# A second result buffer for the early expert tiles, one set of PSUM banks for Mamba, experts and results, and row fetches ahead of weight loads

## Chip, core and metric

The kernel runs on one core of a Trainium2 chip. A core has five engines with queues of their own: TensorE (PE: matmuls, with its weight loads listed as PEld), VectorE (DVE), ScalarE (ACT), GpSimd (POOL) and SyncE (SP), which here issues most of the DMAs. PE writes its products to PSUM, eight banks of 512 float32 columns on 128 partitions; DVE and ACT read them there. The metric is the device time of one execution in microseconds. Names such as L1825 are line numbers of the kernel before.

## What is computed

The input is a float32 image tensor of 2 x 256 x 48 x 48. Layer 0 is a hybrid of a 7 x 7 neighbourhood attention and dynamic depthwise convolutions. Its output is taken as 2 x 2304 = 4608 tokens of 256 features, and layer 1 is a Mamba block followed by a mixture of eight experts, of which each token uses two. The part that matters here, cut from the reference:

```python
t = _to_tokens(x)
t = t + _L1_attn_ref(_ln_t(t), ...)          # Mamba
t = t + _L1_ffn_ref(_ln_t(t), ...)           # experts
x = _from_tokens(t, x)

def _L1_ffn_ref(x, Wg, bg, W1, b1, W2, b2):
    gate_logits = xf @ Wg + bg
    top_w, top_i = jax.lax.top_k(gate_logits, 2)
    top_w = jax.nn.softmax(top_w, axis=-1)
    for e in range(8):
        h = jax.nn.gelu(xf @ W1[e] + b1[e], approximate=False)
        out = out + w_dense[:, e:e + 1] * (h @ W2[e] + b2[e])
```

W1 is 256 x 1024 and W2 1024 x 256 for each expert.

## The kernel before

**Order of the work.** `run` goes through four stages: layer 0, Mamba with the gate, the experts, and the results. Layer 0 and Mamba are put in order by a planner, `Flow`. Each operation is given an engine, a cost, the operations it needs, and the buffers that it takes and frees; `room` tells how many buffers of each kind there are. The planner walks through time with these costs and writes one order for PE, DVE, ACT and SP. POOL's order is kept by `on_pool`. Behind the plan, semaphores make each instruction wait for its data and for its buffer, so the engines run in the planned order but not at planned times. The experts and the results are written as plain loops.

**Mamba and the gate.** 36 chunks of 128 tokens run through Mamba. A finished chunk's tokens lie in `x` on chip; a copy goes to DRAM in `acc` (the keep, L1505), where the experts' rows are added later. The gate works on groups of chunks. For each chunk it normalizes the tokens (L1664) and POOL scatters them, once for each of the two chosen experts, into a table `xs` in DRAM that is sorted by expert (the row puts, L1673, an indirect DMA each). A row holds 256 features, eight weights and the token's number.

**Early tiles.** Before the gate has seen every chunk, the kernel takes the expert with most tokens so far and runs three tiles of 256 of its rows, numbered 0 to 2, beside Mamba (`early_tile`). One tile is: a fetch of its rows (L1762), four PE transposes (L1771), a copy to SBUF (L1787), W1 products in four pairs (L1799), GELU on ACT (L1807), W2 products (L1815) summed in one bank, the sum with the bias on DVE (L1825), the scaling by the expert weight on ACT (L1831), and two scatters that add 128 rows each to `acc`, issued by POOL (L1834). The expert weight comes from POOL (L1775) and DVE (L1783). The tile's input, hidden values and result lie in columns of `x[1]` whose tokens are done with. There is one result buffer (`ey=1` in `room`): columns 768 to 1023.

**Plan of the rest.** When all counts are known, `plan` computes on DVE (L1863 to L1926) which rows and which expert each of the remaining tiles has. Its scratch values lie in `x[1]` from column 1024 on (`begun`).

**Experts.** 33 pair tiles of 256 rows and four single tiles of 128 rows follow (four more singles stand in a branch for unusual counts). Tile i needs `load(i)`, SP's DMAs of 136 KB (`bt`) and 2 MB (`wt`) of weights (L1979, L1981; tile 0 has its weights in `x[0]` already), and `fetch(i)`, SP's DMA of its rows (L1989). The first of them stand on SP's queue in the order load 1, fetch 0, fetch 1, load 2, fetch 2, behind eight DMAs that fill the ends of the table. `turn` transposes the rows on PE (L897), copies them on DVE (`ext`, L899), and takes the token numbers and weights. `up` makes 32 matmuls (L2045) with a GELU per bank (L2049). `down` of a pair tile makes seven products of 128 x 128 blocks (L2083), Strassen's scheme, whose operand sums `ts` and `ss` DVE has made (L2019 to L2034); then ACT copies the first product (L2087), DVE sums the products (L2088 to L2096), ACT scales (L2054), and POOL scatters and adds to `acc` (L2055). A single tile has plain products (L2070).

**Results.** After the last scatter has landed, `acc` is read back in 12 pieces (L2147), transposed on PE (L2158), copied by DVE and ACT (L2161) and written out (L2164).

**PSUM.** Layer 0 has its own pool. Mamba has six banks that the planner hands out (`bank`) and a pool of two for the z products (`zbank`). The experts open two new pools in place of Mamba's: four single banks, and two sets of two banks for the products of `down`. The results open the same two again. A new pool in the place of an old one can be used when the old one's last users are done:

```python
def psum(self, ctx, bank, banks):
    self.ps = self.pool("ps", bank, ctx, space=bass.MemoryType.PSUM)
    self.ps2 = self.pool("ps2", banks, ctx, space=bass.MemoryType.PSUM)
```

Of the kernel before, what the change touches and what calls it, by code (L numbers as in the profile page):

```python
# [31 lines left out]
F32 = mybir.dt.float32  # L32
I32 = mybir.dt.int32
AF = mybir.ActivationFunctionType
# [3 lines left out]
P = 128  # L38
B, C, H, W = 2, 256, 48, 48
N = H * W  # L40
NH = C // P
# [26 lines left out]
NCHUNK = B * NBLK * NJ  # L68
# [5 lines left out]
TR = 256  # L74
# [152 lines left out]
class Kernel:  # L227
# [4 lines left out]
    def pool(self, name, bufs, ctx=None, **kw):  # L232
        return (ctx or self.ctx).enter_context(self.tc.tile_pool(name=name, bufs=bufs, **kw))

    def bank(self):
        return self.ps.tile([P, 512], F32, tag="bank", name="bank")

    def banks(self):
        return self.ps2.tile([P, 2, 512], F32, tag="banks", name="banks")

    def psum(self, ctx, bank, banks):
        self.ps = self.pool("ps", bank, ctx, space=bass.MemoryType.PSUM)
        self.ps2 = self.pool("ps2", banks, ctx, space=bass.MemoryType.PSUM)


    def setup(self):
# [70 lines left out]

    def bank_for(self, key):
        slot = self.flow.slot["bank", key]
        t = self.tiles["bank", key] = self.ps.tile([P, 512], F32, tag=f"bank{slot}", name="bank")  # L320
        return t

    def banks_for(self, key):
# [5 lines left out]
    def layer0(self, ctx):  # L329


        nc, ins = self.nc, self.ins
        self.ps = self.pool("ps", 1, ctx, space=bass.MemoryType.PSUM)
        wts = self.pool("l0w", 1, ctx)
        room = dict(bank=4, banks=2, q=2, prob=3, pt=4, val=3, vout=2, hid=2, place=2)
        self.begin_flow(self.pool("att", 1, ctx), room, self.PACE0, self.LEAD0)
        self.kp = [wts.tile([P, HP, HP], F32, name=f"kp{h}") for h in range(NH)]
        self.xp = {(b, h): wts.tile([P, H, W], F32, name=f"xp{b}{h}") for b in range(B) for h in range(NH)}
        self.prepare(wts)
        self.scale_weights()  # L340
        for b in range(B):
            self.group_norm(b)
            for g in range(-(-H // KG)):
                self.keys(b, g)
            for rb in range(NRB):
                self.queries(b, rb)
            for pair in range(N // (2 * P)):
                self.values(b, pair)
            self.convolutions(b)
            for i in range(NBQ):  # L350
                self.block(b * NBQ + i)
        self.run_flow()
# [560 lines left out]
    def mamba(self, ctx):  # L913

        nc = self.nc
        self.ps = self.pool("ps", 1, ctx, space=bass.MemoryType.PSUM)
        self.zps = self.pool("zps", 2, ctx, space=bass.MemoryType.PSUM)

        room = dict(bank=6, zbank=2, cvbank=2, t=3, xn=2, xc=2, bc=3, cz=2, z=2, btt=2, xd=3, xw=2,
                    mt=4, yi=1, y=4, sq=2, state=3, rd=2, u2=2, ex=1, ext=1, ehid=2, ey=1)
        self.begin_flow(self.pool("m", 1, ctx), room, self.PACE1, self.LEAD1)
        zeros = self.pool("cz", 1, ctx)
        self.cz = [zeros.tile([P, 2, TB], F32, name=f"cz{i}") for i in range(room["cz"])]
        for t in self.cz:
            nc.gpsimd.memset(t, 0.0)
        for k in range(B * NBLK):
            self.norms(k)
            self.project_block(k)  # L930
            self.decays_of(k)
            for c in range(k * NJ, (k + 1) * NJ):
                self.chunk(c)
        first = 0
        for g, n in enumerate(GROUPS):
            self.gate(g, first, n)
            first += n
        self.early_expert(sum(GROUPS[: EARLY + 1]))
        for i in range(NEARLY):
            self.early_tile(i, sum(GROUPS[: EARLY + 1]))  # L940
        self.run_flow()
# [248 lines left out]
    def decays_of(self, k):  # L1190
# [54 lines left out]
        for i in range(NZ):  # L1245
            at = (k, i)

            def gate(i=i, at=at):
                if i == 0:
                    self.large_tile("z", k, [P, NZ, TB])  # L1250
                T["zbank", at] = self.zps.tile([P, 512], F32, tag="zbank", name="zbank")
                self.project(
                    T["zbank", at][:, :TB], lambda h: win[:, h, i * P : (i + 1) * P], lambda h: T["xn", k][:, h, 3:]
                )

            op(("z", at), "PE", 1300, gate, *rows, ("z", (k, i - 1)) if i else None,
               takes=[("zbank", at)] + ([("z", k)] if i == 0 else []), uses=[("xn", k)])
# [483 lines left out]
    def early_tile(self, i, seen):  # L1741
# [4 lines left out]
        w1 = wt[:, : NH * HID].rearrange("p (k o) -> p k o", k=NH)  # L1746
        w2 = wt[:, NH * HID :].rearrange("p (k o) -> p k o", k=NHC)
        late = NCHUNK + 6 + i
        xt, hid, y = (self.x[1][:, :, a * TR : b * TR] for a, b in ((0, 1), (1, 3), (3, 4)))
        free = [(name, c) for c in (NCHUNK // 2 + 6, NCHUNK // 2 + 7) for name in ("u2", "keep")]  # L1750
        sp = [mybir.EngineType.SP]
        puts = [("put", (c, q)) for c in range(seen) for q in range(2)]
        weights = [("ew", (0, q)) for q in range(8)]
# [68 lines left out]
               takes=[("bank", ("ed", i))] if p == 0 else [], uses=[("ehid", (i, p))])  # L1822

        def add():
            self.last_add = vec.tensor_tensor(y, T["bank", ("ed", i)].rearrange("p (j q) -> p j q", j=2),  # L1825
                              bcast(bt[:, NHC : NHC + C], 1, [P, 2, C]), ALU.add)

        op("ea", "DVE", 690, add, ("ed", (i, NHC // 2 - 1)), *free, takes=[("ey", i)], uses=[("bank", ("ed", i))])
        for j in range(2):
            def scale(j=j):  # L1830
                nc.scalar.activation(y[:, j, :], y[:, j, :], AF.Identity, scale=T["eweight", i][:, j : j + 1])  # L1831

            def put(j=j):
                ins = pool.indirect_dma_start(  # L1834
                    self.acc, bass.IndirectOffsetOnAxis(ap=T["etoken", i][:, j : j + 1], axis=0), y[:, j, :],
                    None, compute_op=ALU.add,
                ).ins
                self.tc.declare_no_dep(ins, group="early", reason="a token has one row of an expert")
                self.tc.declare_no_dep(ins, group="late keeps", reason="later chunks have other rows")
                self.tc.add_to_no_dep_group("early", ins)  # L1840

            op(("es", (i, j)), "ACT", 390, scale, ("ea", i), ("eweight", i))
            op(("eput", (i, j)), "POOL", 1500, put, ("es", (i, j)), ("etoken", i), *[("keep", c) for c in range(seen)],
               uses=[("ey", i)])

    def plan(self):

        nc, begun = self.nc, [4 * TR] * NH
        n, k, tid = P, CAP // TR, self.c["tid"]
        tri = self.c["tri"].rearrange("p (a b) -> p a b", a=E)  # L1850

# [91 lines left out]

    def experts(self, ctx):
        nc, ins = self.nc, self.ins
        self.psum(ctx, 4, 2)
        hp = self.pool("eh", 2, ctx)
        ew = self.pool("ew", 3, ctx)
        sp = [mybir.EngineType.SP]
# [111 lines left out]
        def down(i):  # L2061
            wt, bt, hid = *weights[i], hidden[i]
            w2 = wt[:, NH * HID : NH * HID + NHC * C].rearrange("p (k o) -> p k o", k=NHC)
            b2 = bt[:, NHC : NHC + C]
            banks = self.ps2.tile([P, 2, 512], F32, tag="banks", name="po")
            if tiles[i][0] == 1:
                y = hp.tile([P, C], F32, tag="ey", name="ey", bufs=5)
                po = banks[:, 0, :C]
                for c in range(NHC):
                    nc.tensor.matmul(po, lhsT=hid[:, c, :P], rhs=w2[:, c, :], start=c == 0, stop=c == NHC - 1)  # L2070
                nc.vector.tensor_add(y, po, b2)
                finish(i, y, 0)
            else:
                v = sums.pop(i)
                p = {}

                for n, (name, a, w) in enumerate((
                    (1, "a11", "b11"), (7, "s3", "t3"), (2, "a12", "b21"), (4, "a22", "t4"), (5, "s1", "t1"),
                    (6, "s2", "t2"), (3, "s4", "b22"),
                )):  # L2080
                    p[name] = banks[:, n // 4, n % 4 * P : (n % 4 + 1) * P]
                    for c in range(NHC // 2):
                        nc.tensor.matmul(p[name], lhsT=v[a][:, c], rhs=v[w][:, c], start=c == 0, stop=c == NHC // 2 - 1)  # L2083
                y0, y1 = (hp.tile([P, C], F32, tag="ey", name="ey", bufs=5) for _ in range(2))
                p1, u2, u3, u4 = (hp.tile([P, P], F32, tag=f"u{j}", name=f"u{j}", bufs=1) for j in range(4))
                add = nc.vector.tensor_add
                nc.scalar.copy(p1, p[1])  # L2087
                add(y0[:, :P], p[2], p1)  # L2088
                add(u2, p[6], p1)
                add(u3, p[7], u2)  # L2090
                add(u4, p[5], u2)
                add(y1[:, :P], p[4], u3)
                add(y1[:, P:], p[5], u3)
                add(y0[:, P:], p[3], u4)
                for j, y in enumerate((y0, y1)):
                    add(y, y, b2)  # L2096
                    finish(i, y, j)
# [3 lines left out]
        for e in range(E):  # L2101
            fill(e)
        load(0)
        load(1)
        fetch(0)
        fetch(1)
        load(2)
        fetch(2)
        with self.tc.issue_after(self.last_add.ins):
# [26 lines left out]
    def results(self, ctx):  # L2136

        nc = self.nc
        self.psum(ctx, 4, 2)
        op = self.pool("o", 12, ctx)  # L2140

        blocks = []
# [156 lines left out]
```

## Time and profile before

| | |
|---|---|
| median of 3 runs | 1323.94 us (1323.86 to 1324.54) |
| the profiled execution | 1323.21 us, of which the span from first to last instruction is 1321.3 us |
| PE busy | 1237.3 us (94%) |
| DVE, ACT, POOL busy | 930.1, 796.4, 557.2 us |
| mean granted PE clock | 0.979 |

The stages around the change, from the trace's table of windows:

| stretch (us) | what runs there | PE busy | granted clock | DMA share |
|---|---|---|---|---|
| 765.0 to 783.5 | end of the gate, early tiles 1 and 2 | 18.31 | 1.00 | 0.55 |
| 783.5 to 794.5 | early tile 2 | 0.00 | 0.73 | 1.07 |
| 794.5 to 806.0 | early tile 2, hand-over | 9.94 | 0.81 | 0.45 |
| 806.0 to 1236.0 | expert tiles | 429.82 | 1.00 | 0.66 |
| 1236.0 to 1284.0 | last expert tiles | 47.76 | 1.00 | 0.41 |
| 1284.0 to 1293.0 | last sums and scatters | 0.00 | 0.67 | 0.25 |
| 1293.0 to 1321.3 | results | 12.22 | 0.74 | 0.89 |

Times in the trace count from the first instruction. A row of a timeline gives the start, the duration, the engine, the line, the operation with its output and inputs, and in brackets how long the engine stood idle before it and what ended that. The granted clock is the share of full speed at which PE could run. A DMA share of 1 means that the core's sixteen DMA engines were all busy (packets that overlap can take it over 1).

### The profile page before, as it was taken

To read this page: it belongs to the slowest core of one execution; us is meant where nothing else is said; L and a number is where in the kernel's file an instruction comes from. 1 tells how busy PE (TensorE), PEld (TensorE's weight loads), DVE (VectorE), ACT (ScalarE), POOL (GpSimd) and SP (SyncE) were. 2 spreads that over 40 slices of the span, in tenths; PEclk is the share of its full clock that TensorE was granted. 3 is DMA by queue.
4 is the path that set the end of the run, shared out by engine and by line. 5 is a ranking of instruction groups with operands and counts; after the bars stand their busy time and mean duration, and the time that the engine had idled before them with its cause. 6 is when DMAs were issued, how large, how long until landed. Compare 5 with 4: busy or idle time off the path is not lost. (4 is left out here: it accounts for less than half of the span.)

```text
span 1321.3 us, 23603 instructions
## 1 busy us (share of the span) xinstructions
PE 1237.3 (94%) x8072; PEld 984.5 (75%) x8072; DVE 930.1 (70%) x2427; ACT 796.4 (60%) x1957; POOL 557.2 (42%) x769
## 2 busy tenths in 40 slices
PE   4999999996999999999999968999999999999983
PEld 3566766664667766677677757999999999999982
DVE  5899999998577978888878634565556556555642
ACT  2598868897899887987787623333324333332332
POOL 4312130211367798988889852212212221221220
PEclk9999999999899999999999999999999999999997
DMA  8331322210232342426346165667756765775618
GB/s 293 108 102 47 118 72 89 63 49 30 70 93 83 88 139 86 142 80 191 114 137 179 59 213 172 177 193 229 238 176 226 230 210 183 233 236 183 217 33 295
DMA packets 101659, 194.13 MB, mean 147 GB/s; under 512 B 10635, under 2 KB 82652, under 8 KB 96604
## 3 DMA queue, kind: packets, MB, share of 16 engines
q1 hardware_dynamic: 84156, 166.15, 37.3%
q0 software_dynamic: 14400, 19.74, 7.6%
q10 hardware_dynamic: 2980, 6.69, 1.4%
q8 instruction: 66, 1.08, 0.3%
q14 instruction: 57, 0.47, 0.1%
HBM read 154.24 MB, written 43.23 MB: 149 GB/s over the span
## 5 line engine op out<-in xcount | busy, mean ns | idle before, releaser
L2055 POOL DMA_INDIRECT acc<-ey,token x70 | 109.0, 1558 | 371.7 <-ACT ey L2054 331.1
L2045 PE MATMUL bank<-ext,wt 128*128 128x256 f32 (+1 forms) x1152 | 241.3, 368 | 0.0
L2045 PEld LDWEIGHTS bank<-ext,wt 128*128 128x128 f32 x1152 | 207.0, 190 | 25.0
L2049 ACT ACTIVATE hid<-bank,bt 128x256 f32<-128x256 f32 (+1 forms) x288 | 132.3, 461 | 84.9 <-PE bank L2045 80.2
L2087 ACT COPY u<-po 128x128 f32<-128x128 f32 x33 | 8.8, 266 | 205.8 <-PE po L2083 200.0
L676 POOL COPY kp<-kp 128x10 f32<-128x10 f32 (+1 forms) x60 | 24.7, 412 | 179.5 <-DVE kp L669 179.5
L587 DVE SCALAR_TENSOR_TENSOR x<-hid,w2r,x 128x1128 f32<-128x1128 f32 (+3 forms) x72 | 99.9, 1393 | 0.4 <-ACT hid L581 0.2
L2083 PE MATMUL po<-ts,ss 128*128 128x128 f32 x792 | 99.2, 275 | 0.0
L911 PE MATMUL bank<-xn,win 128*128 128x387 f32 x240 | 93.0, 511 | 1.6 <-ACT t L993 1.6
L2083 PEld LDWEIGHTS po<-ts,ss 128*128 128x128 f32 x792 | 93.7, 192 | 0.0
L1123 DVE SCALAR_TENSOR_TENSOR xc<-bank,vec,xc 128x384 f32<-128x384 f32 x144 | 86.6, 611 | 9.2 <-ACT xc L1112 8.6
L1339 ACT ACTIVATE mt<-mt,cum 128x128 f32<-128x128 f32 x288 | 87.7, 393 | 0.0
L795 ACT ACTIVATE prob<-prob,top 128x308 f32<-128x308 f32 x144 | 78.2, 550 | 15.4 <-DVE top L784 15.0
L1673 POOL DMA_INDIRECT xs<-u,rows x72 | 72.5, 1008 | 16.0 <-issue 13.8
L2019 DVE TENSOR_TENSOR ts<-wt 128x512 f32<-128x512 f32 x32 | 22.2, 692 | 80.8 <-PE po L2083 80.8
L2032 DVE TENSOR_TENSOR ss<-hid 128x512 f32<-128x512 f32 x33 | 22.8, 691 | 72.8 <-ACT hid L2049 72.8
L1445 PE MATMUL bank<-wout,y 128*128 128x264 f32 x288 | 71.6, 393 | 1.2 <-DVE yi L1404 1.2
L911 PE MATMUL zbank<-xn,win 128*128 128x384 f32 x192 | 71.0, 491 | 0.3 <-ACT z L1241 0.3
L801 ACT ACTIVATE prob<-prob,rden 128x308 f32<-128x308 f32 x144 | 67.6, 549 | 3.7 <-DVE rden L850 3.7
L577 DVE SCALAR_TENSOR_TENSOR hid<-xp,vec,hid 128x1175 f32<-128x1175 f32 (+1 forms) x48 | 68.4, 1425 | 0.1
L2083 PE MATMUL po<-wt,hid 128*128 128x128 f32 x512 | 67.6, 275 | 0.0
L784 DVE CUSTOM_DVE_ANT_0 prob<-banks,cst 128x308 f32<-128x308 f32 x144 | 61.7, 472 | 4.9 <-PE banks L774 4.6
(324 smaller groups left out, 3017.7 us busy)
## 6 DMA issues: line engine op xcount, KB each, us to landing
wt<-in_We SPq DMA_DIRECT2D x36, 2048.0 KB
mt<-decays SPq DMA_DIRECT2D x36, 512.0 KB
ex<-xs SPq DMA_DIRECT2D x36, 265.0 KB
rd<-decays SPq DMA_DIRECT2D x68, 128.0 KB
val<-vtab SPq DMA_DIRECT2D x72, 110.0 KB
bt<-in_We SPq DMA_DIRECT2D x36, 136.0 KB
vraster<-vout SPq DMA_DIRECT2D x18, 256.0 KB
acc<-x SPq DMA_DIRECT2D x36, 128.0 KB
```

The source lines that it names most:

```text
L577: nc.vector.scalar_tensor_tensor(dst, src, w[:, k : k + 1], dst, ALU.mult, ALU.add)
L587: nc.vector.scalar_tensor_tensor(dst, src, w[:, k : k + 1], dst, ALU.mult, ALU.add)
L795: nc.scalar.activation(t, t, AF.Exp, bias=T["top", c][:, a : a + 1], scale=-1.0, accum_out=T["den", c][:, a : a + 1])
L911: self.nc.tensor.matmul(ps, lhsT=lhs(k), rhs=rhs(k), start=k == 0, stop=k == NH - 1)
L1123: nc.vector.scalar_tensor_tensor(out(), T["bank", ("cv", at)][:, i : i + TB], wc[:, i : i + 1], out(), ALU.mult, ALU.add)
L1339: nc.scalar.activation(t, t, AF.Relu, bias=at_s, scale=-1.0)
L1445: nc.tensor.matmul(ps[:, : C + E], lhsT=T["y", c][:, m, :], rhs=self.l1["wout"][:, m, :], start=m == 0, stop=m == NZ - 1,)
L1673: ins = nc.gpsimd.indirect_dma_start(self.xs, bass.IndirectOffsetOnAxis(ap=of("rows")[:, i, q : q + 1], axis=0), T["u2", g][:, i, :], None,)
L2045: nc.tensor.matmul(ps[:, :rows], lhsT=w1[:, k, c * P : (c + 1) * P], rhs=xt[:, k, :], start=k == 0, stop=k == NH - 1,)
L2049: nc.scalar.activation(hid[:, c, :], ps[:, :rows], AF.Gelu, bias=bt[:, c : c + 1])
L2055: put = nc.gpsimd.indirect_dma_start(self.acc, bass.IndirectOffsetOnAxis(ap=token[:, j : j + 1], axis=0), y, None, compute_op=ALU.add)
L2083: nc.tensor.matmul(p[name], lhsT=v[a][:, c], rhs=v[w][:, c], start=c == 0, stop=c == NHC // 2 - 1)
```

## The change

The change has three parts.

1. **Two result buffers.** `room` has `ey=2`. The planner gives each early tile one of two slots in `x[1]`, columns 768 to 1023 or 1024 to 1279; the tiles take them in the order first, second, first. Tiles 1 and 2 also need chunks 26 and 27, whose columns the second slot covers, to be done with. The plan's scratch begins at column 1280.
2. **One set of banks.** Mamba's pool now lives to the end, with the two `zbank` as banks of it that the planner hands out. A list `used_banks` keeps the banks in the order in which they were last used. The experts take the four that were used longest ago for transposes and `up`, and the other four for `down`: two for a pair tile, one for a single tile. The results go on with the same four. The two banks of a pair tile are now two tiles and no longer one of twice the size. The first four products of `down` (1, 7, 2, 4) lie in the first, the other three (5, 6, 3) in the second, as before.
3. **Order on SP.** Fetch 0, fetch 1, load 1, load 2, fetch 2.

In the order of the instructions, PE's is the same up to the results. On DVE the weight L1783 of tile 2 moves one place ahead; behind tile 2's sum comes `ext` of the first expert tile, ahead of its `own`, `token` and first `ts`; and in each pair tile the first sum of products (L2088) comes ahead of the next tile's first two `ts`. A memset of the plan moves back by some places. In the results one block changes places with its neighbour on PE and ACT.

```diff
+    def next_bank(self, ring, name):
+        tag = ring.pop(0)
+        ring.append(tag)
+        return self.ps.tile([P, 512], F32, tag=tag, name=name)
+
     def bank(self):
-        return self.ps.tile([P, 512], F32, tag="bank", name="bank")
...
-    def psum(self, ctx, bank, banks):
-        self.ps = self.pool("ps", bank, ctx, space=bass.MemoryType.PSUM)
-        self.ps2 = self.pool("ps2", banks, ctx, space=bass.MemoryType.PSUM)
+        return self.next_bank(self.ring, "bank")
+
+    def share_banks(self):
+
+        self.ring, self.sums = self.used_banks[:4], self.used_banks[4:]
...
         slot = self.flow.slot["bank", key]
-        t = self.tiles["bank", key] = self.ps.tile([P, 512], F32, tag=f"bank{slot}", name="bank")
+        t = self.tiles["bank", key] = self.next_bank([f"bank{slot}"], "bank")
+        self.used_banks = [tag for tag in self.used_banks if tag != f"bank{slot}"] + [f"bank{slot}"]
...
-        self.ps = self.pool("ps", 1, ctx, space=bass.MemoryType.PSUM)
-        self.zps = self.pool("zps", 2, ctx, space=bass.MemoryType.PSUM)
+        self.ps = self.pool("ps", 1, space=bass.MemoryType.PSUM)
+        self.used_banks = ["zbank0", "zbank1"]
...
-                    mt=4, yi=1, y=4, sq=2, state=3, rd=2, u2=2, ex=1, ext=1, ehid=2, ey=1)
+                    mt=4, yi=1, y=4, sq=2, state=3, rd=2, u2=2, ex=1, ext=1, ehid=2, ey=2)
...
-                T["zbank", at] = self.zps.tile([P, 512], F32, tag="zbank", name="zbank")
+                T["zbank", at] = self.next_bank([f"zbank{self.flow.slot['zbank', at]}"], "zbank")
...
-        free = [(name, c) for c in (NCHUNK // 2 + 6, NCHUNK // 2 + 7) for name in ("u2", "keep")]
+        free = [(name, NCHUNK // 2 + c) for c in (6, 7, 8, 9)[: 2 + 2 * (i > 0)] for name in ("u2", "keep")]
...
         def add():
+            at = 3 + self.flow.slot["ey", i]
+            y = T["ey", i] = self.x[1][:, :, at * TR : (at + 1) * TR]
             self.last_add = vec.tensor_tensor(y, T["bank", ("ed", i)].rearrange("p (j q) -> p j q", j=2),
...
-        nc, begun = self.nc, [4 * TR] * NH
+        nc, begun = self.nc, [5 * TR] * NH
...
-        self.psum(ctx, 4, 2)
+        self.share_banks()
...
-            banks = self.ps2.tile([P, 2, 512], F32, tag="banks", name="po")
+            banks = [self.next_bank(self.sums, "po") for _ in range(tiles[i][0])]
...
-                    p[name] = banks[:, n // 4, n % 4 * P : (n % 4 + 1) * P]
+                    p[name] = banks[n // 4][:, n % 4 * P : (n % 4 + 1) * P]
...
         load(0)
-        load(1)
         fetch(0)
         fetch(1)
+        load(1)
         load(2)
         fetch(2)
...
     def results(self, ctx):
 
         nc = self.nc
-        self.psum(ctx, 4, 2)
```

## Prediction

> **What bounds the kernel now.** I read the page first: PE is busy 1237.3 us of a span of 1321.3 us, so what can be won is idle PE time and slow PE time. Then the table of windows (columns: busy time and instructions of PE, PE loads, DVE, ACT, POOL; then granted clock, DMA share, GB/s), cut at the stages around the diff:
>
> ```profile
> 765.00:783.50 18.50, 18.31 (x86) 15.45 (x85) 8.23 (x52) 7.02 (x14) 13.55 (x17) 1.00 0.55 176
> 783.50:794.50 11.00, 0.00 (x0) 0.00 (x0) 0.89 (x3) 1.30 (x4) 2.21 (x3) 0.73 1.07 363
> 794.50:806.00 11.50, 9.94 (x36) 7.90 (x36) 2.01 (x5) 2.81 (x7) 2.69 (x3) 0.81 0.45 149
> 806.00:1236.00 430.00, 429.82 (x2911) 402.33 (x2912) 248.13 (x643) 151.27 (x354) 98.38 (x63) 1.00 0.66 207
> ```
>
> From 806 on PE is never idle at full clock: the 37 expert tiles are bound by PE. Ahead of it lies an empty stretch of 11 us, followed by a slow one. The timelines of PE, ACT, DVE and POOL there say why (start, duration, instruction, and in brackets the idle time before it with what ended it):
>
> ```profile
> 794.52 3.78 PE L1815 MATMUL bank<-wt,x 128*128 128x256 f32 x8 [11.09 <-ACT x L1807]
> 804.72 0.63 PE L897 MATMUL bank<-cst,ex 128*128 128x128 f32 x4 [0.89 <-issue]
> ...
> 793.20 0.91 ACT L1831 ACTIVATE x<-x,eweight 128x256 f32<-128x256 f32 x2 [15.74 <-DVE x L1825]
> 794.01 1.18 ACT L1807 ACTIVATE x<-bank,wt 128x256 f32<-128x256 f32 x3
> ...
> 781.85 0.17 DVE L1783 TENSOR_REDUCE eweight<-eown 128x2 f32<-128x16 f32 x1 [9.45 <-POOL eown L1775]
> 783.56 0.17 DVE L1925 TENSOR_SCALAR x<-x 128x8 int32<-128x8 f32 x1
> 792.47 0.69 DVE L1825 TENSOR_TENSOR x<-bank,wt 128x512 f32<-128x512 f32 x1 [8.74 <-DMA acc<-x,etoken]
> 803.92 0.69 DVE L1825 TENSOR_TENSOR x<-bank,wt 128x512 f32<-128x512 f32 x1 [10.76 <-PE bank L1815]
> ...
> 781.98 1.64 POOL L1834 DMA_INDIRECT acc<-x,etoken  x1 [0.17 <-issue]
> 783.92 1.58 POOL L1834 DMA_INDIRECT acc<-x,etoken  x1 [0.30 <-issue]
> ```
>
> Read backwards: PE needs early tile 2's GELUs (L1807); on ACT these stand behind tile 1's scaling (L1831); that needs tile 1's sum (L1825 at 792.47); that writes the only result buffer, which is free once tile 0's two scatters (L1834) have landed. POOL issues them at 781.98 and 783.92, behind its row puts.
>
> **Part 1, two result buffers.** Tile 1 takes the other buffer. Its sum still stands on DVE behind the expert weight L1783 (781.85, waiting for POOL) and the plan's last operation, which starts at 783.56 and ends at 783.73; its matmuls were done before PE's last work ended at 794.52-11.09=783.43. So the sum starts at 783.73 and not 792.47: 8.74 us. ACT's scaling, its GELUs and PE follow as before (2.05 us from sum to PE): PE resumes at 785.78, idle 2.35 us instead of 11.09. What is late next is POOL: the weight L1783 behind the row puts. Moving the plan's scratch by 256 columns makes its memset wait for tokens of the last chunk (L1664, done at 767.1); DVE is idle from 772 to 781.8, which hides that; without this cover it would cost about 0.5 us.
>
> **The clock.** The windows (same columns) around two other gaps and around this one:
>
> ```profile
> 556.53:559.95 3.42, 1.38 (x10) 0.69 (x9) 3.35 (x4) 3.10 (x10) 3.40 (x4) 1.00 0.14 51
> 559.95:563.36 3.41, 3.41 (x16) 2.46 (x15) 2.03 (x4) 1.66 (x4) 3.41 (x6) 0.50 0.02 5
> ...
> 781.81:785.23 3.42, 1.62 (x8) 1.09 (x6) 1.74 (x13) 0.00 (x0) 2.95 (x3) 1.00 0.81 219
> 795.47:798.88 3.41, 3.41 (x9) 2.66 (x8) 0.00 (x0) 0.09 (x1) 1.61 (x2) 0.50 1.02 359
> ```
>
> The clock was 0.50 from 788.64 to 798.88, so PE ran 798.88-794.52=4.36 us at half speed (8 matmuls of L1815 in 3.78 us): 2.18 us lost, which goes with the stall. A new gap of 2.35 us may bring its own. [...] Bounds 0 and 3.41/2=1.7 us; I take 1.7, as the rows nearest in length do. Net of the clock 2.18-1.7=0.48; with the rule, 2.18.
>
> **Part 2, one set of banks.** At the hand-over PE's first transposes (L897, 804.72) wait for tile 2's sum (803.92, 0.69 us), because the new pool needs every old bank free. With the shared set they need only the row fetch and POOL's L1775. After tile 2's last matmul at about 803.84 they would take 0.60 beside the sum; DVE copies ext (L899, from 805.44 to 806.13) directly behind the sum (own, token and the first ts move behind it) and ends at about 805.25: 0.88 us. Per tile, the copy of the first product (L2087) now needs only the first bank's matmuls, so it and the first sum L2088 run while PE fills the second. Beside PE's unbroken work this is worth nothing, except at the last tile: DVE's L2089 can start as soon as PE is done (about 1283.90) and not at 1284.36: 0.46 us, all on the path through the last scatters to the results.
>
> ```profile
> 1283.85 0.27 ACT L2087 COPY u<-po 128x128 f32<-128x128 f32 x1 [5.83 <-PEq L2129]
> 1284.36 0.28 DVE L2089 TENSOR_TENSOR u<-po,u 128x128 f32<-128x128 f32 x1
> ```
>
> New waits: DVE's first sum now stands ahead of ts and waits for ACT and for its result buffer. Mamba's zbank goes from a pool's rotation to the planner's slots, two of each: nothing. In the results stage PE, ACT and DVE swap one block; the DMA share there is 0.89, so the copies are hidden: nothing, or 0.5 us either way (the length of one 0.68 us copy at most).
>
> **Part 3, fetches first.** SP issues fetches 0 and 1 ahead of load 1. The queue was bt at 781.84, wt at 782.38, fetches from 783.69. Fetch 0 must wait for the last row put (issued 780.47), so it goes at about 783 and load 1 some 2.6 us later than before. Cover for the weights: load 1 was wanted at 820.05 and will be near 809, and the DMA windows show two loads finished by 800. Cover for the fetches is tile 2: PE wants fetch 0 at about 793, and behind the weights it landed near 792. So the move costs nothing, gains nothing, and secures 1 us of margin that the earlier stages eat up.
>
> **Sum.** 8.74+0.48+0.88+0.46=10.56. The profiled execution took 1323.21 us (span 1321.3 plus 1.9 around it), 0.73 below the median 1323.94. 1323.21-10.56=1312.65; on the median 1313.4.
>
> **Rivals.**
> - *The stall moves to tile 2* (0.15). Tile 2's sum takes tile 0's buffer again, so it waits for the same scatters, wanted at about 793 (9.1 us after the second one's issue at 783.92). This row has their flight:
>
> ```profile
> DMA to landing us min/median/max: 4.7/8.8/11.8
> ```
>
>  The median is in time; the maximum lands at 795.7, 2.7 us late, with perhaps another half-clock window (1.7): 1316 to 1318. For it: load 1 now runs beside them later than before. Against it: the fetches, of equally small packets, go first and the scatters get most of theirs done beside them.
> - *The first buffer was not what held it* (0.05): the sum of tile 1 also sits behind L1783; were it held by another wait until 792, only part 2 remains: 1323.9-1.3=1322.6. The row names the scatter, against it.
> - *No half-clock window from the new gap* (0.25, within the forecast's range): 1311.7.
> - *Slower* (0.03): DVE's new order. The first sum waits for its result buffer ahead of ts, and PE's second product needs ts about 4 us after ts ends now. If the scatter frees the buffer over 4 us later than ts needs it, each of 37 tiles pays; 10.6 us are eaten at 0.29 us a tile, and 0.4 us a tile gives 1328. Against it: five buffers, two used per 13.6 us tile, are free for about 27 us, and the scatters of the expert stage land in 5.3 us (10.3 at most).
>
> **Numbers.** The forecast mechanism has 0.77 (half-clock window 0.52, none 0.25), the rivals 0.15, 0.05 and 0.03. The likeliest is 1313.4. Low end: 1311.7 less the 0.7 us that separates runs, 1310.8. High end: 1317.5, into the first rival. A measurement tells 0.2% (2.6 us) from no change: faster 0.92 (forecast and first rival), same 0.05, slower 0.03.
>
> **What would show it.** PE's gap at 783.4 of 2 to 3 us, ended by ACT's GELU; tile 1's sum near 783.7 with no DMA wait; tile 2's sum near 793 released by PE (right) or by the scatter (first rival); the first L2045 stretch starting between 794.4 and 796.1 (without and with a half-clock window); no PE idle from there to the end; the last L2089 directly behind PE; whether a 0.50 clock stands at 785 to 792. A gain under 8 us, or over 13, would prove the sum wrong.

## The result and the profile after

The changed kernel takes 1315.85 us in the median of four runs (1315.56 to 1317.14), the kernel before 1323.9 us: a ratio of 0.9941, 95% interval 0.9923 to 0.9958. The gain is 8.05 us (interval 5.6 to 10.2); I had forecast 10.56 (1313.4 us, range 1310.8 to 1317.5). The profiled execution took 1316.04 us, with a span of 1314.3 us against 1321.3.

Line numbers below are those of the changed kernel: the sum L1825 is now L1830, the weight L1783 is L1786, the copy of a tile's input L1787 is L1790, W1 and W2 products are L1802 and L1818, GELU L1810, scaling L1837, scatter L1840, row puts L1676, fills L1972, fetches L1995, the experts' transposes L900, `ext` L902, and their W1 products L2051.

The table of windows of the changed kernel, at the stretches shown before (same columns):

```profile
765.00:783.50 18.50, 12.52 (x52) 10.08 (x51) 8.32 (x54) 6.03 (x12) 13.38 (x16) 0.91 0.51 169
783.50:794.50 11.00, 9.25 (x43) 7.84 (x42) 0.69 (x1) 3.35 (x8) 4.36 (x3) 1.00 0.92 269
794.50:806.00 11.50, 10.55 (x52) 9.08 (x51) 4.85 (x13) 4.61 (x10) 3.24 (x2) 1.00 1.00 351
806.00:1236.00 430.00, 430.00 (x2913) 402.47 (x2912) 251.45 (x647) 152.94 (x358) 97.36 (x63) 1.00 0.66 209
```

The empty stretch of 11 us has filled up. But the stretch ahead of it, full before (18.31 us busy), now has only 12.52 us of PE work and a clock of 0.91. The timelines of PE, ACT and DVE say where that went:

```profile
772.18 1.89 PE L1818 MATMUL bank<-wt,x 128*128 128x256 f32 x8
778.88 3.54 PE L1802 MATMUL bank<-x,wt 128*128 128x256 f32 x8 [4.81 <-issue]
782.21 2.08 PE L1818 MATMUL bank<-wt,x 128*128 128x256 f32 x8
786.03 1.99 PE L1818 MATMUL bank<-wt,x 128*128 128x256 f32 x8 [1.75 <-ACT x L1810]
...
799.77 7.17 PE L2051 MATMUL bank<-ext,x 128*128 128x256 f32 x32 [0.94 <-DVE ext L902]
...
778.24 0.59 ACT L1790 COPY x<-bank 128x512 f32<-128x512 f32 x1 [8.51 <-remote]
778.72 0.85 ACT L1810 ACTIVATE x<-bank,wt 128x256 f32<-128x256 f32 x2
785.50 0.84 ACT L1810 ACTIVATE x<-bank,wt 128x256 f32<-128x256 f32 x2 [5.93 <-PE bank L1818]
...
785.53 0.69 DVE L1830 TENSOR_TENSOR x<-bank,wt 128x512 f32<-128x512 f32 x1 [2.54 <-PE bank L1818]
798.42 0.69 DVE L1830 TENSOR_TENSOR x<-bank,wt 128x512 f32<-128x512 f32 x1 [12.20 <-PE bank L1818]
799.03 0.68 DVE L902 COPY ext<-bank 128x512 f32<-128x512 f32 x1
```

What was forecast is there: neither sum names a DMA, tile 2's sum is released by PE, and `ext` follows it directly. What was not forecast is the first ACT row. The copy of tile 2's input writes the one input buffer, so it waits for tile 1's last W1 matmuls. Those end at 772.34 by PE's records, but PE's semaphore event (the trace's record of the signal that lets a waiting instruction go) is seen only at 778.22, and ACT starts 0.02 us later. PE stands for 4.81 us, a half-clock window follows (779.16 to 782.58 at 0.50), and the GELU at 785.50 and the sum at 785.53 wait in the same way for matmuls recorded as done at 782.4 and 784.3. The sum so comes 1.8 us later than forecast, on an execution that was 0.76 us early by then, and PE's two gaps are 6.56 us together where one of 2.35 was forecast. In the profile of the kernel before, from which the forecast was made, no PE event ahead of the results is late by 0.6 us.

From tile 2's transposes to the first L2051 the stage took 38.92 us before (767.26 to 806.18) and takes 33.27 us now (766.50 to 799.77): 5.65 us gained where my terms for it make 10.10 (8.74+0.48+0.88). The rest of the 7.1 us of span: 0.76 ahead of the stage, nothing in the expert tiles (477.58 us from the first L2051 to the end of the last product of `down`, in both), 0.67 behind them.

### The profile page after: what moved, and what is told of

The parts are those of the page before. It is cut to its first block, busy times and chain, and to the rows that moved or that the text cites. A ratio compares the mean times of both kernels' runs of the same rounds, so it can differ in the third digit from the quotient of the medians.

```text
span 1314.3 us, 23601 instructions
## 1 busy us (share of the span) xinstructions
PE 1232.6 (94%) x8072; PEld 981.6 (75%) x8072; DVE 930.9 (71%) x2427; ACT 797.9 (61%) x1957; POOL 557.2 (42%) x769
## 4 chain that ended last, share of the span: by engine, by line
PE 40%; POOL 10%; DMA 5%; issue 3%; ACT 3%; DVE 3%; SPq 0%; ACTq 0%; DVEq 0%; POOLq 0%
PE bank L2051 17%; PE po L2089 14%; DMA acc<-ey,token 4%; POOL xs L1676 3%; POOL sq L1455 1%; PE bank L914 1%; POOL y L1440 1%; PE bank L1818 1%; PE bank L900 1%; PE zbank L914 1%; POOL y L1422 1%; PE bank L1802 1%; PE bank L1448 1%; PE po L2076 1%; DMA out<-o 1%
## 5 line engine op out<-in xcount | busy, mean ns | idle before, releaser
L2051 PE MATMUL bank<-ext,wt 128*128 128x256 f32 (+1 forms) x1152 | 241.3, 368 | 0.0
L2051 PEld LDWEIGHTS bank<-ext,wt 128*128 128x128 f32 x1152 | 207.0, 190 | 25.0
L2089 PE MATMUL po<-ts,ss 128*128 128x128 f32 x792 | 99.2, 275 | 0.0
L2089 PEld LDWEIGHTS po<-ts,ss 128*128 128x128 f32 x792 | 93.7, 192 | 0.0
L1676 POOL DMA_INDIRECT xs<-u,rows x72 | 72.6, 1009 | 16.1 <-issue 14.4
L2089 PE MATMUL po<-wt,hid 128*128 128x128 f32 x512 | 67.6, 275 | 0.0
L2089 PEld LDWEIGHTS po<-wt,hid 128*128 128x128 f32 x512 | 62.3, 192 | 0.1
```

The source lines that it names most:

```text
L1676: ins = nc.gpsimd.indirect_dma_start(self.xs, bass.IndirectOffsetOnAxis(ap=of("rows")[:, i, q : q + 1], axis=0), T["u2", g][:, i, :], None,)
L2051: nc.tensor.matmul(ps[:, :rows], lhsT=w1[:, k, c * P : (c + 1) * P], rhs=xt[:, k, :], start=k == 0, stop=k == NH - 1,)
```

## The experiments

Theory at the start: the late copy is an accident of one execution or one chip, and the sum of the prediction holds without it. Rival: the new order brings it about. Runs of one group shared a chip and the runs of the kernel before.

**First chip: the change, its parts.** Parts undone or done alone:

```diff
 e2   kernel before, with ey=2, free, add(), begun = 5*TR of the diff
 e3   kernel before, with next_bank, share_banks, used_banks of the diff
 e4   changed kernel:
-        fetch(0)
-        fetch(1)
         load(1)
+        fetch(0)
+        fetch(1)
```

> The changed kernel once more, unchanged. In its first profile tile 2's input copy on ACT (L1790) began at 778.24, 6 us after the matmuls that it waits for, and PE stood 4.81 us and then ran at half clock. Theory (the delay belongs to the new order of things in this stage): a copy that starts 4 us or more after its matmuls and a PE gap of 4 to 6 us near 774 to 779 again, and 1315.5 to 1316.5 us. Rival (an accident of that one execution): the copy within 1 us of its matmuls (772 to 773), PE without a gap before tile 1's sum, and either 1313 to 1314 us or another place where 2.5 us are missing.

> The kernel before with part 1 alone (two result buffers). My sum gives 8.74 us of stall and 0.48 of clock: 9.2, so 1314.7 us. If the late input copy comes with the second buffer, 2.5 us of it are given back: about 1317.2. If the first rival (the stall moves to tile 2) holds once the row fetches stand behind the weight load: 1318 to 1320. The hand-over must look as in the kernel before (PE's first transposes behind tile 2's sum).

> The kernel before with part 2 alone (shared banks). My sum gives 0.88 us at the hand-over and 0.46 us at the last tile: 1322.6 us, with the 11 us gap of PE at 783.4 still there. Rival (DVE's new order costs in the expert tiles): no gain, 1324 or more, and an expert stretch longer than in the kernel before.

> The changed kernel with load 1 ahead of fetches 0 and 1 again (parts 1 and 2 alone). My step: part 3 is worth nothing by itself, so 1315.9 us, the same as the changed kernel within 0.5 us. Rival: with the weights first, the rows of the first expert tile land after PE wants them (near 793 to 799), or the scatters of tile 0 land late and hold tile 2's sum: 1317 to 1319 us, with a DMA wait at one of these two places.

| | median us | ratio to before (95%) | stage, tile 2's transposes to first L2051 |
|---|---|---|---|
| before | 1323.11 | | 38.92 (profile shown above) |
| e1, whole change | 1310.69 | 0.9903 (0.9879 to 0.9927) | 28.65 |
| e2, buffers | 1314.04 | 0.9925 (0.9903 to 0.9947) | 29.73 |
| e3, banks | 1321.37 | 0.9981 (0.9971 to 0.9991) | 38.13 |
| e4, no fetch order | 1311.19 | 0.9908 (0.9886 to 0.9929) | 27.63 |

Here the change is worth 12.4 us by the medians (interval 9.7 to 16.0). The timelines of PE, ACT and DVE of e1:

```profile
777.25 3.62 PE L1802 MATMUL bank<-x,wt 128*128 128x256 f32 x16
783.08 3.68 PE L1818 MATMUL bank<-wt,x 128*128 128x256 f32 x8 [2.22 <-ACT x L1810]
...
770.54 0.59 ACT L1790 COPY x<-bank 128x512 f32<-128x512 f32 x1 [2.63 <-PE bank L1802]
...
779.26 0.17 DVE L1786 TENSOR_REDUCE eweight<-eown 128x2 f32<-128x16 f32 x1 [8.92 <-POOL eown L1778]
781.05 0.68 DVE L1830 TENSOR_TENSOR x<-bank,wt 128x512 f32<-128x512 f32 x1
791.98 0.69 DVE L1830 TENSOR_TENSOR x<-bank,wt 128x512 f32<-128x512 f32 x1 [10.25 <-PE bank L1818]
```

This is the picture of the prediction: the copy 0.04 us behind its matmuls (768.61+1.89=770.50), PE busy up to one gap of 2.22 us (2.35 forecast), the sum behind the weight that waits for POOL. The rival of e1 held, in its stronger form: the late copy does not belong to the change as such. By the medians e2 and e3 give 9.1 and 1.7 us (intervals of 2.9 and 1.3 us either way) where the sum has 9.2 and 1.34. e4's median is 0.5 us from e1's, far inside intervals of 3 us either way; in its trace the rows land late by 0.45 us, which is all that the trace shows of part 3:

```profile
793.44 0.63 PE L900 MATMUL bank<-cst,ex 128*128 128x128 f32 x4 [0.45 <-DMA ex<-xs]
```

**Second chip: does it come back, and what holds the sum.**

```diff
 e6, e7 (e7 with load 1 ahead of fetches 0 and 1), and e8 on the kernel before:
-        op("eweight", "DVE", 170, weight, ("eown", i))
+        op("eweight", "DVE", 170, weight, ("eown", i), ("ea", 1) if i == 2 else None)
```

`("ea", 1)` is tile 1's sum; the planner then puts tile 2's weight behind it.

> The changed kernel a third time. In its second profile the input copy on ACT began 0.1 us after its matmuls, PE had no gap before tile 1's sum, and the stage went as the sum said, so the late copy of the first profile was no lasting part of the change. Theory: it was an accident of that execution; this time the copy follows its matmuls within 1 us, PE's gap ahead of tile 2's second half is 2.2 to 2.3 us, and the gain against the kernel before is 10 to 13 us. Rival: on some chips it comes in every execution; then a gain of 7.5 to 9 us with the late copy in the profile.

> The changed kernel with tile 2's expert weight (L1786 on DVE, which waits for POOL) placed behind tile 1's sum; nothing else moves but the plan's operations that had stood behind it. Theory (with a second buffer the sum is held only by the weight and by POOL's row puts): the sum starts when its matmuls end, near 777.5, PE's gap of 2.2 us is gone and with it the half-clock window that some executions had: 2.2 to 3.9 us faster than the changed kernel. Rival (something else holds the sum or PE at almost the same time, such as ACT's order or the row fetch of the first expert tile): under 1 us, with a new wait in its place.

> The same as the run before it (weight behind the sum), but with load 1 ahead of fetches 0 and 1 again. My step: behind the weights the first rows land about 0.5 us after PE wants them in the changed kernel's timing; with the gap gone PE wants them 2.2 to 3.9 us earlier, so PE should wait 2.5 to 4.5 us at its transposes (L900) with a DMA named, and the whole gain of that edit is lost: as fast as the changed kernel within 0.5 us. Rival (the order on SP is worth nothing even then): as fast as the run before it.

> The kernel before, one result buffer, with the same edit (tile 2's weight behind tile 1's sum). Theory (the buffer, that is tile 0's scatters, held the sum): no change, 0 within 0.5 us, with the sum still near 792 and a DMA wait ahead of it. Rival (the sum was held by the weight and POOL, and the buffer came only just behind it): 5 us faster or more.

Here the unchanged change is worth 4.2 us: ratio 0.9972 (0.9961 to 0.9983). The rival of e5 held, and went further than it said: the copy is 4.5 us behind its matmuls (776.42), and PE's gaps are 3.44 and 3.26 us. (The profiled execution, 1322.76 us, is the slowest of its seven; their median is 1317.61.) PE and ACT of e5:

```profile
781.59 2.95 PE L1802 MATMUL bank<-x,wt 128*128 128x256 f32 x8 [3.44 <-issue]
790.26 3.78 PE L1818 MATMUL bank<-wt,x 128*128 128x256 f32 x8 [3.26 <-ACT x L1810]
...
780.96 0.58 ACT L1790 COPY x<-bank 128x512 f32<-128x512 f32 x1 [7.21 <-remote]
```

e6 (0.9973, 0.9964 to 0.9981) and e7 (0.9966, 0.9958 to 0.9974) show the late copy too (4.6 and 7.4 us behind its matmuls) and change nothing; so e6 failed as a test of the weight, and e7 as a test of the row fetches, because PE now came too late to want rows early. e8 is the telling one. It is 1.0008 of the kernel before (0.9999 to 1.0016), and shows in the timelines of PE, ACT and DVE how the kernel before lives with the same delay:

```profile
780.61 3.78 PE L1799 MATMUL bank<-x,wt 128*128 128x256 f32 x8 [7.71 <-issue]
...
793.24 1.99 PE L1815 MATMUL bank<-wt,x 128*128 128x256 f32 x8 [1.19 <-ACT x L1807]
...
779.97 0.59 ACT L1787 COPY x<-bank 128x512 f32<-128x512 f32 x1 [11.37 <-issue]
...
791.20 0.69 DVE L1825 TENSOR_TENSOR x<-bank,wt 128x512 f32<-128x512 f32 x1 [17.85 <-DMA acc<-x,etoken]
```

The copy comes 8.8 us behind its matmuls (769.28+1.89), PE stands 7.71 us, and then hardly stands at the sum: 1.19 us instead of 11.09. The sum still waits for tile 0's scatters until 791.20. With one buffer the scatters set the end of the stage, and 7.7 us of delay ahead of it cost nothing. With two buffers they are on the path. (The kernel before is no slower on the two chips with late events, 1321.8 and 1322.3 us, than on the two without, 1323.1 and 1321.2.) It also settles what held the sum in the kernel before: the buffer, not the weight.

**Third chip: what delays the events.** In the profiles with a late copy some semaphore events are missing from the trace. In that of the result PE has 1203 events for 1218 instructions that send one, DVE 2063 for 2153, ACT 1254 for 1284 and POOL 441 for 448; in that of the kernel before PE has 1185 for 1185, DVE 2088 for 2087, ACT 1286 for 1284 and POOL 450 for 448. Nearly all of the gaps lie in five stretches, in the result 465 to 491, 535 to 556, 601 to 629, 667 to 690 and 751 to 784 us, and ahead of the results PE events come over 0.6 us late only there or just behind: 0.9 us at 479, 0.8 at 616, 1.8 at 683, 1.9 at 756, and those of 778.22, 785.42 and 785.51 named above. POOL issues its 72 row puts in these stretches (464 to 496, 533 to 556, 601 to 632, 667 to 690, 734 to 781). Not all of the lateness lies beside them: in the profile of the result, the last row put is issued by 780.70 and the events of 785.42 and 785.51 are still up to 3.0 us late, beside tile 0's two scatters (781.24 and 783.18). In e1 to e4 the copy starts 0.04 us behind its matmuls. So e9 takes the last 12 row puts out of the stretch, and e10 takes away one of the waits that the delay hits. The unchanged change was not run on this chip.

```diff
 e9
-        op("g10", "DVE", 175, ..., ("row", (g, 1)), ("row", (g, 2)))
+        op("g10", "DVE", 175, ..., ("row", (g, 1)), ("row", (g, 2)), ("ea", 1) if g >= 5 else None)
 e10, with the edit of e6
-                    mt=4, yi=1, y=4, sq=2, state=3, rd=2, u2=2, ex=1, ext=1, ehid=2, ey=2)
+                    mt=4, yi=1, y=4, sq=2, state=3, rd=2, u2=2, ex=1, ext=2, ehid=2, ey=2)
...
+            T["ext", i] = self.x[1][:, :, :TR] if i != 1 else self.small.tile([P, NH, TR], F32, tag="xt1", name="xt1", bufs=1)
...
```

> A test of the cause, not a faster version: in the changed kernel the last 12 row puts (L1676, chunks 30 to 35) are made to wait for tile 1's sum, since DVE makes their row numbers behind it. In the profiles with the late copy, semaphore events are missing only in the five stretches in which POOL issues row puts, and PE's events come late only there. Theory (row puts delay the semaphores on such a chip): with no row put between 766 and the sum, the copy L1790 starts within 1 us of its matmuls and PE has no gap before tile 1's sum, while the late events of the earlier row-put stretches (479, 616, 683 us) are still there; late events may now come behind the sum. Rival (the fills or something else in this stretch): the copy again 4 to 7 us late with PE idle 3 us or more near 774. On a chip without late events at 479 to 683 the run cannot tell. The rows of the first expert tile land later by some 12 us, so the time is about 5 us above the changed kernel's.

> The changed kernel with tile 2's weight behind tile 1's sum, and with a second input buffer for tile 1, so that tile 2's copy (L1790) no longer waits for tile 1's last W1 matmuls. On a chip with punctual semaphores: no PE gap at 781, 2.2 to 3.9 us faster than the changed kernel, so 0.987 to 0.989 of the kernel before. On a chip with late semaphores: the copy starts behind its transposes near 767 to 771, the first PE gap shrinks by the 1.7 us of W1 matmuls that can now run in it, and a later gap stays where GELU waits for PE: about 2 us faster than the changed kernel there (0.995 to 0.996 of the kernel before). Rival: the second buffer moves the late event to the next GELU and gains nothing there.

e9, timelines of PE, ACT, DVE and POOL:

```profile
775.15 1.89 PE L1802 MATMUL bank<-x,wt 128*128 128x256 f32 x8
776.88 3.62 PE L1818 MATMUL bank<-wt,x 128*128 128x256 f32 x16
801.34 1.09 PE L900 MATMUL bank<-cst,ex 128*128 128x128 f32 x4 [10.48 <-issue]
...
773.63 0.58 ACT L1790 COPY x<-bank 128x512 f32<-128x512 f32 x1 [2.72 <-PE bank L1802]
...
778.81 0.69 DVE L1830 TENSOR_TENSOR x<-bank,wt 128x512 f32<-128x512 f32 x1 [0.95 <-PE bank L1818]
...
780.38 1.02 POOL L1676 DMA_INDIRECT xs<-u,rows  x1 [9.05 <-DVE rows L1659]
795.71 1.59 POOL L1840 DMA_INDIRECT acc<-x,etoken  x1 [0.30 <-issue]
```

The theory held: this chip has late events in the earlier stretches (0.9, 0.8 and 1.1 us at 480, 617 and 684), but with no row put between 764 and 780 the copy is 0.04 us behind its matmuls and PE has no gap over 0.3 us before tile 1's sum. The eight fills, still there at 767 to 774, did not delay the copy by themselves here. But the row puts at 780 to 795 brought only one late event, of 0.8 us (tile 2's sum, 791.68), so row puts alone do not always do it. On POOL's queue tile 0's scatters moved too, from 781.24 and 783.18 to 767.42 and 769.37 (the one at 795.71 is tile 1's), so for the later delay (the GELU and the sum) e9 does not part row puts from scatters. The rows land late, as foreseen (fetch 0 goes out at 798.7; PE stands 10.48 us), and the time is 0.9991 of before (0.9983 to 1.0).

e10: 0.9979 (0.9969 to 0.9989), and its rival held as far as the trace goes; what it gains over the unchanged change on this chip was not measured. PE and ACT (its L1792, L1805, L1813 and L1821 are the copy, the W1 products, the GELU and the W2 products):

```profile
785.32 3.78 PE L1821 MATMUL bank<-wt,x 128*128 128x256 f32 x8 [8.00 <-ACT x L1813]
...
768.19 0.59 ACT L1792 COPY x<-bank 128x512 f32<-128x512 f32 x1
...
774.80 0.84 ACT L1813 ACTIVATE x<-bank,wt 128x256 f32<-128x256 f32 x2 [5.28 <-remote]
784.79 0.84 ACT L1813 ACTIVATE x<-bank,wt 128x256 f32<-128x256 f32 x2 [9.15 <-remote]
```

The copy is early, and the next thing that waits for PE, the GELU, takes the delay in its place (its events come 3.0 and 7.4 us late): one gap of 8.00 us.

**Fourth chip: the fills taken out instead.**

```diff
 e11, with the edit of e6
-        for e in range(E):
-            fill(e)
         load(0)
         fetch(0)
-        fetch(1)
         load(1)
+        for e in range(E):
+            fill(e)
+        fetch(1)
```

> The changed kernel with tile 2's weight behind tile 1's sum, and with the eight fills of the table (L1972 on SP, at 765 to 774) moved behind fetch 0 and load 1, so that in this stretch the row puts have no fills beside them. In the run before, the fills without the row puts gave no late event, and the row puts without the fills (780 to 795) gave only one of 0.8 us. Theory A (both together are needed on a chip with late events): copy within 1 us of its matmuls, no PE gap before tile 1's sum, and 3 to 6 us faster than the changed kernel on the same chip. Theory B (the row puts alone do it, where PE's events meet them): the copy late by 3 us or more again and within 1.5 us of the changed kernel. On a chip without late events: 2.2 to 3.9 us faster than the changed kernel, from the gap at 781 alone.

> The changed kernel on the same chip, for comparison. On a chip with late events at 479, 616 and 683 us: the late copy and two PE gaps of 3 to 5 us, and 0.994 to 0.997 of the kernel before. On a chip without: one gap of 2.2 us, and 0.989 to 0.992.

Neither profile has a late event in this stretch (the copy starts 0.04 us behind its matmuls in both), so whether row puts need fills beside them to do harm stays open. e12, the unchanged change, is 0.9925 of before (0.9909 to 0.9941), with the copy on time, one gap of 2.24 us and a stage of 27.16 us. In e11 the weight edit does what e6 was to show, and the moved fills spoil it; timelines of PE, DVE and SP:

```profile
779.71 3.62 PE L1802 MATMUL bank<-x,wt 128*128 128x256 f32 x16
783.16 1.89 PE L1818 MATMUL bank<-wt,x 128*128 128x256 f32 x8
...
805.22 1.09 PE L900 MATMUL bank<-cst,ex 128*128 128x128 f32 x4 [6.43 <-DMA ex<-xs]
...
778.18 0.69 DVE L1830 TENSOR_TENSOR x<-bank,wt 128x512 f32<-128x512 f32 x1 [3.70 <-PE bank L1818]
...
802.39 0.41 SPq L1995 DMA_DIRECT2D ex<-xs  x1
```

The sum comes at 778.18, ahead of the weight (781.71), and the gap is gone: a stage of 24.47 us, 2.7 less than e12's. But fetch 1, which must follow the fills, is issued only at 802.39 (the fills went out from 786.73 on, beside the first weights), PE waits 6.43 us for its rows, and the half clock that follows (804.05 to 810.88, where the four transposes take 1.09 us and not 0.60) makes it 9.3 us (486.90 us of expert tiles instead of 477.58). e11 is 0.9954 of before (0.9939 to 0.9969), slower than e12. The weight edit with the fills in place was not run on a chip of this kind.

## Why the prediction was right, and the step that failed

The mechanism was right: the buffer held the sum, and with a second one the empty stretch closed. That the time also lay in the range is in part luck. The range reached up to 1317.5 us for another reason, the first rival, which did not occur; and the gain that it allows, 6.4 to 13.1 us, holds the 8.05 us of this chip but not the 4.2 us of the second. (Its low end is also 0.2 us off: 1311.7-0.7 is 1311.0 and not 1310.8.) The gain was 2.5 us short because of one assumption.

- **Part 1, 8.74 us.** Right where PE's events were punctual. The stage shrinks from 38.92 to 27.16 us in e12, 11.8 us, where my terms without a half-clock window make 8.74+2.18+0.88=11.80; with one (e1) it shrinks by 10.27, where they make 10.10. The failed step is "its matmuls were done before PE's last work ended" with "what is late next is POOL". I read it from a trace in which everything ahead of the sum was on time, and did not ask what delays the 11 us stall had been covering. On the chip of the result it was ACT's copy that was late next, by 6 us, behind an event of PE; of 10.10 us 5.65 were left in the stage.
- **The clock, 1.7 us charged.** Right in size, and by chance in this execution: its half-clock window came from the 4.81 us gap, not from the 1.75 us one. The 1.7 was an estimate, half of one 3.41 us window. In the kernel before, the gaps of 2.04 us (ended 559.12) and 2.10 us (ended 739.99) were each followed by a window at 0.50; the window 781.81 to 785.23, with 1.62 us busy, was followed by one at 1.00. No run shows a length of gap that decides between the 0.48 and the 2.18 of the forecast: of the four profiles with a gap of 2.22 to 2.24 us, e1 and e2 had the window, e4 and e12 did not.
- **Part 2, 0.88+0.46 us.** Right: e3 gained 1.74 us, 0.79 of it in the stage. In the changed kernel DVE's L2095 (L2089 before) starts 0.03 us behind PE's end at 1277.35 (1276.29+1.06):

```profile
1276.29 1.06 PE L2089 MATMUL po<-wt,ss 128*128 128x128 f32 x8
1277.38 0.29 DVE L2095 TENSOR_TENSOR u<-po,u 128x128 f32<-128x128 f32 x1 [2.03 <-PE po L2089]
```

  Before, it started at 1284.36, 0.60 us behind PE's end at 1283.76 (806.18+477.58), so this alone is 0.57 us; I had put PE's end at 1283.90. From PE's last product to the end there are 36.3 to 36.9 us in the eleven profiles with shared banks and 37.2 to 37.6 in the three without, 0.8 on average where I had 0.46.
- **Part 3, nothing.** No run speaks against it: the medians of e1 and e4 are 0.5 us apart, with intervals of 3 us either way. The margin that I put at 1 us was -0.45 us in e4.
- **Rivals.** The stall did not move to tile 2: its sum names PE in every profile with two buffers. The slower case was not seen: the expert tiles take 477.58 us in every profile but three (e8 479.26 and e9 479.98, which begin at half clock: 0.46 us a matmul where e1 has 0.22, and e11). That the buffer was not the holder is excluded by e8.

The chip as the cause of late events is inferred: within a group all profiles agreed (six of six with the row puts in place on the second and third chip and in the result, none of six on the other two), but each chip was met only once. A rival stands untested: the events that are late and those that are missing from the trace lie in the same stretches, so the recording of the trace may itself be part of the delay. Every run on record has a span and a clock from its own trace, so none tells the time without the recording.

## What to carry to other kernels

A stall that is taken away had covered the delays ahead of it (7.71 us in e8). Before counting its length as gain, list what the engines wait for during it and how much of each wait is margin, and measure on more than one chip: here the same change was worth 4.2 us on one (interval 2.2 to 5.2) and 12.4 us on another (9.7 to 16.0). If a wait of one engine for another is removed and the delay lies in the events themselves, as in e10, it can move to the next such wait (there a gap of 8.00 us).

## What the hardware did that was not expected

**Late events.** In the result and on two of the four chips behind it, events of PE reached ACT and DVE 0.8 to 7.4 us late beside POOL's row puts and tile 0's scatters (by the start of the copy 8.8 us in e8, where no event is seen), and events of PE, DVE, ACT and POOL are missing from the trace of the same stretches (in the result 1203, 2063, 1254 and 441 for 1218, 2153, 1284 and 448 instructions).

**What a half-clock window follows.** From 420 to 1250 us of these traces it goes by PE's busy time in windows of 3.41 us on a fixed grid, not by the length of a gap. The grid shows in the half-clock stretches: from 700 to 1290 us each lasts 3.41, 6.83, 10.24 or 13.65 us, and their starts lie whole multiples of 3.41 apart (before: 740.85, 788.64 and 1286.99, 14 and 146 windows). Two gaps of equal length (2.22 and 2.23 us), in e1 and then e4, on each trace's own grid:

```profile
779.71:783.12 3.41, 1.19 (x7) 0.71 (x5) 1.88 (x12) 1.36 (x4) 2.89 (x2) 1.00 0.46 62
783.12:786.53 3.41, 3.41 (x8) 2.79 (x9) 0.00 (x0) 1.00 (x3) 3.01 (x2) 0.50 1.11 278
```

```profile
780.56:783.97 3.41, 3.03 (x15) 2.32 (x13) 1.83 (x15) 0.00 (x0) 2.98 (x4) 1.00 0.64 153
783.97:787.38 3.41, 1.56 (x7) 1.41 (x8) 0.50 (x1) 2.36 (x6) 3.00 (x2) 1.00 0.88 338
```

In e1 the gap lies in one window (1.19 us busy) and the next is at 0.50; in e4 it is split over two and the clock stays at 1.00. Over the fourteen profiles, from 420 to 1250 us, all 33 full-clock windows with at most 1.38 us of PE work were followed by a half-clock one, and of those with 1.5 us or more only four (1.69 to 1.92 us). Outside that stretch busy time does not tell it alone: in the kernel before, the window 187.90 to 191.31, with 3.34 us of PE work, was followed by one at 0.50. The mean granted clock also goes with much of the spread between runs: over 27 runs of the kernel before on one chip, from 1320.1 to 1327.8 us, 0.001 of it went with 0.9 us (0.83 of the variance), on the other three with 0.5 to 0.7 us (0.45 to 0.71).
